# A scan's two terms: summed by GpSimd and turned once, with two operations moved by a step

## The chip, the cores and the metric

One core of a Trainium2 chip runs the kernel. The metric is device time in microseconds (us) of one execution. The engines are TensorE (PE; its weight loads are listed apart as PEld), VectorE (DVE), ScalarE (ACT), GpSimd (POOL) and SyncE (SP, which issues the DMAs).

## The reference

Four images of 128 channels and 64 x 64 pixels pass two layers. Only what matters here is kept:

```
# layer 0: state-space scan, per channel d (two chunks of 64 in one tile of 128 rows), 16 states n, 4096 pixels t
h[d, n] = exp(delta[d, t] * A[d, n]) * h[d, n] + delta[d, t] * B[n, t] * xin[d, t]
y[d, t] = sum over n of h[d, n] * C[n, t]
out     = (y + D * xin) * silu(z) @ out_proj        # then a norm, a projection, a residual
...
# layer 1: attention (4 heads of 32) over 4096 tokens, then a top-2 mixture of 8 experts
att = softmax(q @ k.T / sqrt(128)) @ v
```

The sum over the 16 states is where the change lies.

## The kernel before

**Tiles.** An image is 8 blocks of 512 pixels. A block has two halves p (two chunks each, 128 rows), and a half has 16 states, taken two at a time. A pair of states of one half is a unit; there are 4 x 8 x 2 x 8 = 512 units. VectorE runs both states of a unit in one scan over 1025 columns (`scan`), with the start of the second state put between them.

**The loop.** The main loop (from line 1291) goes in steps, which the code calls slots: two for each unit, so 1,024, and then more until the attention and the closing rows are through. The order of every engine's instructions is the order in which the loop issues them: line 445 is the helper that records each operation and ties it to the one before it on its engine, which is why nearly all rows of the profile have that line. A step issues:

- in an even step VectorE's product of rows and du into h (`driven`) and the scan of the unit; in an odd step `read`, which multiplies h by the rows of C into hc (128 x 2 x 512, two buffers);
- on ScalarE one half of the next unit's decays da (`decayed`, an exponential of 128 x 512), in odd steps the copy of one state into the next unit's h (`carried`), and two exponentials pT of 128 x 1024 for the attention (`exponentials`);
- on TensorE four score matmuls sc and, for the group of the step before, the weighted sums av (`weighted`);
- half steps of two lanes, X and Y, which hold all the rest as generators: each `yield` ends a half step. Y holds the norms, the convolution and the inputs of a block (`inputs`); X holds `closed` (what follows the scans of a block: projection, norm, keys, queries and values) and `finished` (task "out": attention's closing and the experts). Both keep their own order. A task "out" may start only in steps 2 to 17 of each 32; `closed` is put at the head of X's list by `summed_up` when the second half of its block is summed.

**The sum over states.** hc holds the terms of two states. Each term is turned by TensorE (`turned_on`, four transposes of 128 x 128 that accumulate in one PSUM tile y), so that TensorE adds up 16 terms. The first term of a unit is due one step after `read`, the second two steps after (line 1313 and 1314). After the last, ScalarE copies y to yT, a step later `turned_back` turns it back into the same PSUM buffer, and at once `summed_up` lets VectorE combine it with the input (xin <- xin, dsk, y) and GpSimd multiply it by the gate (zs).

**The state copy.** `kept` (ScalarE, 128 x 2) stores both last states of a unit's scan for the next block, 16 units later. It is issued at the end of the even step, the one that issues the scan.

**The start.** Attention needs finished blocks; its first group comes in step 80. ALONE is step 64 (two blocks).

Of the kernel before, what the change touches and what calls it, by code (L numbers as in the profile page):

```python
# [36 lines left out]
def conv_mamba_attn_moe_kernel(ctx: ExitStack, tc: tile.TileContext, t: dict):  # L37
# [401 lines left out]
    class Queue:  # L439
# [7 lines left out]
    tensor, vector, scalar, gpsimd, sync = (  # L447
        Queue(e) for e in (nc.tensor, nc.vector, nc.scalar, nc.gpsimd, nc.sync)
    )
# [14 lines left out]
    def flush():  # L464
        for entry in outgoing:
            entry[0] -= 1
            if entry[0] == 0:
                sync.dma_start(out=entry[1], in_=entry[2])
        outgoing[:] = [entry for entry in outgoing if entry[0]]
# [292 lines left out]
    def kept(unit, h):  # L762
        b, i, p, n = unit
        if i < NB - 1:
            scalar.copy(states[b % 2][:, p, n : n + 2], h[:, :, BLK - 1])

    def driven(unit, h, w):
        b, i, p, n = unit
        du = in_of[b, i, p][3]
        vector.tensor_mul(h[:, :, 0:BLK], w, du[:, None, :].to_broadcast([P, 2, BLK]))  # L770

    def scan(unit, h, da):

        b, i, p, n = unit
        h, da = (a.rearrange("p k q -> p (k q)")[:, 0 : 2 * BLK + 1] for a in (h, da))
        vector.tensor_tensor_scan(
            out=h, data0=da, data1=h, initial=states[b % 2][:, p, n : n + 1],
            op0=ALU.mult, op1=ALU.add,
        )

    def read(h, w):
        hc = mix.tile([P, 2, BLK], F32, name="hc", bufs=2)
        vector.tensor_mul(hc, w, h[:, :, 0:BLK])
        return hc

    def scanned(b, i, p, y):
        xin, zs, delta, du, bcd = in_of.pop((b, i, p))
        vector.scalar_tensor_tensor(xin, xin, dsk, y, ALU.mult, ALU.add)
        gpsimd.tensor_mul(zs, xin, zs)
        gated[b, i, p] = zs  # L790

    def turned_on(y, term, first, last):

        for j in range(NT):
            s = slice(j * P, (j + 1) * P)
            tensor.matmul(
                y[:, s], lhsT=term[:, s], rhs=ident, start=first and j == 0,
                stop=last and j == NT - 1, is_transpose=True,
            )

    def summed_up(b, i, p, y):
        scanned(b, i, p, y)
        done.add(("scan", b, i, p))
        if p == 1:
            lanes["X"].appendleft((("closed", b, i), closed(b, i), []))

    def turned_back(b, i, p, yT):
        y = ps_y.tile([P, BLK], F32, name="y")
        for j in range(NT):
            tensor.transpose(y[:, j * P : (j + 1) * P], yT[:, j * P : (j + 1) * P], ident)  # L810
        summed_up(b, i, p, y)

    vst = side.tile([P, NH, NT, 2 * DH], F32, name="vst")
    gpsimd.memset(vst[:, :, :, DH:], 1.0)
# [184 lines left out]
    sums, partial, total, inverse, later = [None], {}, {}, {}, deque()  # L999

    def exponentials(group):
        pTs = []
        for v, sc in group[3]:
            pT = att.tile([P, 2, BLK], F32, name="pT", bufs=4)
            scalar.activation(pT, sc, AF.Exp, scale=ATT_SCALE)
            pTs.append((v, pT))
        return *group[:3], pTs, *group[4:]
# [174 lines left out]
    lanes, done, running = {"X": deque(), "Y": deque()}, set(), {}  # L1182
# [3 lines left out]
    def advance(lane, second):  # L1186

        if inside[lane] != second:
            return False
        while True:  # L1190
            if lane not in running:

                tasks = lanes[lane] if lanes[lane] or slot < END else lanes["X"]
                if not tasks or not all(k in done for k in tasks[0][2]):
                    return False

                if (
                    tasks[0][0][0] == "out" and slot < END + 4
                    and not 2 <= slot % (2 * NST) < NST + 2
                ):  # L1200
                    return False
                key, stages, _ = tasks.popleft()
                running[lane] = key, stages(lane) if callable(stages) else stages
            key, stages = running[lane]
            try:
                next(stages)
                inside[lane] = not second
                return True
            except StopIteration:
                assert not second  # L1210
                done.add(key)
                del running[lane]

    def until(key):
        while key not in done:
            flush()
            count = len(done)
            moved = [
                advance(*half) for half in (("X", True), ("Y", False), ("Y", True), ("X", False))
            ]  # L1220
            assert any(moved) or len(done) > count, key
# [7 lines left out]
    X, Y = lanes["X"], lanes["Y"]  # L1229
# [9 lines left out]
    for k in range(-2, len(blocks)):  # L1239
        if 0 <= k:  # L1240
            b, i = blocks[k]
            Y.append((("in", b, i, 1), inputs(b, i, 1), [("scan", *blocks[k - 1], 1)] if k else []))
        if k + 2 < len(blocks):
            b, i = blocks[k + 2]
            if k + 2 == 0 or i > 0:
                upper(k + 2)
        if 0 <= k + 1 < len(blocks):
            b, i = blocks[k + 1]
# [10 lines left out]
    left = [None]  # L1259
# [8 lines left out]
    END = 2 * len(units)  # L1268

    ALONE = NB // 2 * NST  # L1270
    rows, due, closing, y_of = {}, deque(), deque(), {}
    h_of, slot = {}, 0

    def fetch(*wanted):
        for ahead, k in wanted:
            if ahead < len(units):
                until(("in", *units[ahead][:3]))
                rows[ahead, k] = fetched(units[ahead], k)

    def prepared(ahead, k):  # L1280
        if ahead < len(units):
            decayed(units[ahead], decays[ahead % 2], k)
            if k:
                h_of[ahead] = carried(units[ahead])

    def ends(unit):
        return unit[3] == NST - 2

    waiting = None

    while slot < END or due or closing or waiting or left or later or lanes["X"] or running:
        at, odd = divmod(slot, 2)
        flush()
        if slot == 0:
            fetch((0, 0), (0, 1), (1, 0))
            prepared(0, 0)
            prepared(0, 1)
        fetch((at + 2, 0) if odd else (at + 1, 1))
        unit = units[at] if at < len(units) else None
        prepared(at + 1, odd)  # L1300
        if unit and not odd:
            h = h_of.pop(at)
            driven(unit, h, rows.pop((at, 0)))
        advance("X", True)
        group = next(groups, None)
        if group:
            group = exponentials(group)
        if unit and not odd:
            scan(unit, h, decays[at % 2])
        if unit and odd:  # L1310
            hc = read(h, rows.pop((at, 1)))
            late = slot >= ALONE and unit[3] == 0
            due.append((slot + 1 + late, unit, 0, hc[:, 0, :], False))
            due.append((slot + 2, unit, 1, hc[:, 1, :], ends(unit)))
        advance("Y", False)
        while closing and closing[0][0] <= slot:
            turned_back(*closing.popleft()[1:])
        while due and due[0][0] <= slot:
            _, (b, i, p, n), k, term, done_with = due.popleft()
            first = n == 0 and k == 0  # L1320
            if first:
                y_of[b, i, p] = ps_y.tile([P, BLK], F32, name="y")
            turned_on(y_of[b, i, p], term, first, done_with)
            if done_with:
                yT = mix.tile([P, BLK], F32, name="yT")
                scalar.copy(yT, y_of.pop((b, i, p)))
                closing.append((slot + 1, b, i, p, yT))
        advance("Y", True)
        if unit and not odd:
            kept(unit, h)  # L1330
        if waiting:
            weighted(waiting)
        waiting = group
        advance("X", False)
        while later and later[0][0] <= slot:
            next(later.popleft()[1])
        slot += 1
# [113 lines left out]
```

## Time and profile before

| | us |
|---|---|
| three runs | 5374.57, 5390.83, 5391.15; median 5390.83 |
| profiled execution, its own time | 5380.67 |
| its span, first to last instruction | 5378.9 |
| first scan, last scan (start, from the span's start) | 101.1, 4787.7 |
| ScalarE idle before the state copies, all 448 | 416.3 |
| scan, mean of 512 | 2.491 |
| products h and hc, mean of 512 each | 1.382, 1.369 |
| GpSimd's adds avs <- avs, prev, mean of 96 | 1.594 |

How to read the profile: rows of groups give line, engine, operation, out<-in by tile names, count, busy time, mean of one, and the idle time of that engine just before them with what ended it. The view of waits sums those idle times by pairs (who waited for whom: total us, times, longest us). The view by windows gives busy us of each engine in stretches of the span, then the granted TensorE clock (1.00 is full), the DMA engines' share and GB/s. The timeline lists instructions in order of time: start, us, engine, line, operation, tiles, count. Matmuls are pipelined and their ends are modelled, so intervals between starts say more than their busy time. POOL's spans are rough.

### The profile page before, as it was taken

How to read it: one execution, taken by the hardware profiler on the slowest of the kernel's cores; microseconds unless marked ns; L12 is line 12 of the kernel's file. 1: busy time of each engine (PE TensorE's matmuls, PEld its weight loads, DVE VectorE, ACT ScalarE, POOL GpSimd, SP SyncE). 2: the span in 40 equal slices, each digit the busy share in tenths (PEclk: the TensorE clock that was granted, in tenths of full speed). 3: DMA queues.
4: the chain of work that ended last, by engine and by line, in shares of the span. 5: the costliest groups of instructions: out<-in, count | busy, mean ns of one | idle time of the engine just before them, and what ended most of it. 6: DMA issues, size and time to landing. Idle time of an engine off the chain costs nothing. (4 is left out here: it accounts for less than half of the span.)

```text
span 5378.9 us, 64061 instructions
## 1 busy us (share of the span) xinstructions
PE 4850.0 (90%) x21066; PEld 2366.3 (44%) x21066; DVE 3757.2 (70%) x5123; ACT 3926.8 (73%) x6117; POOL 1525.0 (28%) x1091
## 2 busy tenths in 40 slices
PE   4556898999999999999999999999999999999997
PEld 2333444444444444444444444444444444444443
DVE  4888767777777778877778778777777877751332
ACT  3456777888777788788877788787777787766553
POOL 2333233333322224223322324333322232310100
PEclk7677899999999999999999999999999999999998
DMA  3556567667666667666766667666766676655532
GB/s 95 176 186 208 197 205 242 231 228 240 232 209 215 218 218 258 225 223 233 257 216 213 217 221 251 233 207 240 270 205 202 207 237 218 239 191 174 174 138 70
DMA packets 451702, 1131.71 MB, mean 210 GB/s; under 512 B 51985, under 2 KB 135330, under 8 KB 451362
## 3 DMA queue, kind: packets, MB, share of 16 engines
q1 hardware_dynamic: 450194, 1126.74, 62.4%
q8 instruction: 169, 2.77, 0.2%
q14 instruction: 171, 1.40, 0.1%
q10 hardware_dynamic: 1168, 0.80, 0.0%
HBM read 967.12 MB, written 143.39 MB: 206 GB/s over the span
## 5 line engine op out<-in xcount | busy, mean ns | idle before, releaser
L445 ACT ACTIVATE pT<-sc 128x1024 f32<-128x1024 f32 x2048 | 1985.7, 1024 | 637.2 <-PE sc L445 635.5
L445 PE MATMUL av<-pT,v 128*64 128x512 f32 x8192 | 2011.1, 612 | 16.7 <-ACT avs L445 16.4
L445 PE MATMUL sc<-qs,ks 128*128 128x512 f32 x4096 | 1316.7, 440 | 134.4 <-ACT pT L445 82.1
L445 DVE TENSOR_TENSOR_SCAN h<-da,state,h 128x1025 f32<-128x1025 f32 x512 | 1275.5, 2491 | 198.2 <-ACT h L445 168.9
L445 PEld LDWEIGHTS sc<-qs,ks 128*128 128x128 f32 x4096 | 705.6, 192 | 835.6 <-ACT pT L445 376.0
L445 PEld LDWEIGHTS av<-pT,v 128*64 128x64 f32 x8192 | 503.4, 138 | 824.7 <-issue 780.0
L445 ACT ACTIVATE da<-delta,amat 128x512 f32<-128x512 f32 x1024 | 747.9, 731 | 4.5 <-POOL delta L445 2.6
L445 DVE TENSOR_TENSOR h<-rows,du 128x1024 f32<-128x1024 f32 x512 | 707.8, 1382 | 53.0 <-POOL du L445 28.5
L445 DVE TENSOR_TENSOR hc<-rows,h 128x1024 f32<-128x1024 f32 x512 | 700.9, 1369 | 18.2 <-PE y L445 4.4
L445 PE MATMUL y<-ident,hc 128*128 128x128 f32 x4096 | 639.5, 285 | 64.3 <-DVE hc L445 56.9
L445 PEld LDWEIGHTS y<-ident,hc 128*128 128x128 f32 x4096 | 523.5, 147 | 269.2 <-issue 116.7
L445 POOL TENSOR_TENSOR rsX<-rsX,mhalf 128x4 f32<-128x4 f32 x92 | 232.7, 2530 | 843.1 <-DVE shiftX L445 843.1
L445 ACT ACT_TABLE_LOAD x319 | 409.3, 1283 | 18.1 <-PE ps_Y L445 13.5
L445 POOL TENSOR_TENSOR rsY<-rsY,mhalf 128x4 f32<-128x4 f32 x100 | 171.5, 1715 | 795.7 <-DVE shiftY L445 795.7
L445 ACT COPY state<-h 128x2 f32<-128x2 f32 x448 | 87.8, 196 | 416.3 <-DVE h L445 412.4
L445 POOL TENSOR_TENSOR avs<-avs,prev 128x512 f32<-128x512 f32 x96 | 153.0, 1594 | 660.2 <-ACT avs L445 612.6
L445 POOL TENSOR_TENSOR zs<-xin,zs 128x512 f32<-128x512 f32 x64 | 105.0, 1640 | 806.5 <-DVE xin L445 797.2
L445 POOL TENSOR_SCALAR du<-e 128x512 f32<-128x512 f32 x64 | 130.3, 2035 | 554.6 <-ACT e L445 554.6
L445 DVE TENSOR_TENSOR share<-share,xf 128x1024 f32<-128x1024 f32 x128 | 177.9, 1390 | 150.9 <-DMA share<-sharesX 124.9
L445 PE MATMUL ps_X<-share,w_ew 128*128 128x512 f32 x432 | 214.5, 619 | 1.7
L445 DVE TENSOR_TENSOR res<-res,ps_X 128x512 f32<-128x512 f32 x108 | 73.4, 679 | 178.9 <-PE ps_X L445 126.9
L445 ACT ACTIVATE xt<-ps_Y,shiftY,rsY 128x128 f32<-128x128 f32 x380 | 143.0, 466 | 67.9 <-POOL shiftY L445 60.7
(238 smaller groups left out, 4415.9 us busy)
## 6 DMA issues: line engine op xcount, KB each, us to landing
rows<-bcd SPq DMA_DIRECT2D x1024, 512.0 KB
ks<-kd SPq DMA_DIRECT2D x192, 512.0 KB
qs<-qd SPq DMA_DIRECT2D x161, 512.0 KB
share<-sharesX SPq DMA_DIRECT2D x108, 512.0 KB
v<-vd SPq DMA_DIRECT2D x192, 256.0 KB
ks<-kd SPq DMA_DIRECT2D x128, 256.0 KB
avd<-avs SPq DMA_DIRECT2D x96, 256.0 KB
prev<-avd SPq DMA_DIRECT2D x96, 256.0 KB
```

The costliest lines, as they stand in the source:

```text
L445: return lambda *args, **kw: queued(op(*args, **kw))
```

## The change

From step 64 on, GpSimd adds the second term of hc to the first, in place, right after `read`, and only the sum is turned, two steps after `read` (three for the first unit of a half). Before step 64 both terms are turned as they were, with the first unit's two steps later. `kept` moves from the end of even steps to the end of odd ones. `turned_back` no longer calls `summed_up`; the loop calls it in the following step, after `driven` and ahead of lane X. Lane Y, which takes from X's list once the units are through, leaves a `closed` to X.

```diff
@@ turned_back
             tensor.transpose(y[:, j * P : (j + 1) * P], yT[:, j * P : (j + 1) * P], ident)
-        summed_up(b, i, p, y)
+        return b, i, p, y
@@ advance
                 tasks = lanes[lane] if lanes[lane] or slot < END else lanes["X"]
+                if tasks and lane == "Y" and tasks[0][0][0] == "closed":
+                    return False
@@ the main loop
-    waiting = None
+    waiting, summing = None, None
...
             driven(unit, h, rows.pop((at, 0)))
+        if summing:
+            summed_up(*summing)
+            summing = None
         advance("X", True)
...
             hc = read(h, rows.pop((at, 1)))
-            late = slot >= ALONE and unit[3] == 0
-            due.append((slot + 1 + late, unit, 0, hc[:, 0, :], False))
-            due.append((slot + 2, unit, 1, hc[:, 1, :], ends(unit)))
+            late = 2 * (unit[3] == 0)
+            if slot < ALONE:
+                due.append((slot + 1 + late, unit, 0, hc[:, 0, :], False))
+                due.append((slot + 2, unit, 1, hc[:, 1, :], ends(unit)))
+            else:
+                gpsimd.tensor_add(hc[:, 0, :], hc[:, 0, :], hc[:, 1, :])
+                due.append((slot + 2 + late // 2, unit, 0, hc[:, 0, :], ends(unit)))
         advance("Y", False)
         while closing and closing[0][0] <= slot:
-            turned_back(*closing.popleft()[1:])
+            summing = turned_back(*closing.popleft()[1:])
...
-        if unit and not odd:
+        if unit and odd:
             kept(unit, h)
```

More of the change, by code (lines that the diff above doesn't have):

```diff
@@ L1287, in ends @@
         return unit[3] == NST - 2
-    waiting = None
-    while slot < END or due or closing or waiting or left or later or lanes["X"] or running:
+    waiting, summing = None, None
+    while (
+        slot < END or due or closing or summing or waiting or left or later or lanes["X"] or running
+    ):
         at, odd = divmod(slot, 2)
```

## The prediction

> **What bounds the kernel now.** First the busy time by engine for the whole span, then the same busy times by stretch, because a mean hides stages with different limits.
>
> ```profile
> PE 4850.0 (90%) x21066; PEld 2366.3 (44%) x21066; DVE 3757.2 (70%) x5123; ACT 3926.8 (73%) x6117; POOL 1525.0 (28%) x1091
> ```
>
> ```profile
> core 0: us, PE busy (x) PEld busy (x) DVE busy (x) ACT busy (x) POOL busy (x), PEclk, DMA share, GB/s
> 100.00:323.00 223.00, 118.68 (x426) 72.45 (x426) 185.44 (x193) 112.83 (x225) 75.63 (x49) 0.67 0.51 171
> 323.00:700.00 377.00, 282.02 (x1156) 152.83 (x1156) 290.45 (x330) 247.57 (x432) 122.52 (x84) 0.84 0.62 204
> 700.00:1266.00 566.00, 530.31 (x2358) 255.87 (x2355) 407.28 (x472) 462.25 (x714) 186.80 (x129) 0.98 0.68 227
> 1266.00:4788.00 3522.00, 3329.12 (x14823) 1627.05 (x14822) 2698.26 (x3579) 2768.70 (x4327) 1081.15 (x741) 0.98 0.67 227
> ```
>
> Columns after the stretch: its length, busy us of PE, PEld, DVE, ACT, POOL. The reader is to see three stages. Until 323 us VectorE leads (185 of 223) and TensorE is half idle. To 700 us they cross. From there TensorE is busy 94%: it is the bound of 4,100 us. In the stretch 1266 to 4788, 370 pairs of scan states take 9.52 us each: 9.00 of TensorE, 7.29 of VectorE, 7.48 of ScalarE. After 4788 us (the last scan) only attention and the closing rows remain.
>
> **What a turn is worth on TensorE.** A turn of one term is four transposes. The group table puts 640 us on 4,096 of them, 0.62 us for four, but matmuls overlap. The tail's timeline, TensorE alone, has steps with a turn and one without:
>
> ```profile
> 4801.48 1.21 PE L445 MATMUL sc<-qs,ks 128*128 128x512 f32 x4
> 4802.52 0.60 PE L445 MATMUL y<-ident,yT 128*128 128x128 f32 x4
> 4803.05 1.94 PE L445 MATMUL av<-pT,v 128*64 128x512 f32 x8
> 4804.92 1.21 PE L445 MATMUL sc<-qs,ks 128*128 128x512 f32 x4
> 4806.06 1.94 PE L445 MATMUL av<-pT,v 128*64 128x512 f32 x8
> ```
>
> Scores to weighted sum: 1.57 us with a turn, 1.14 without. Over the whole trace the medians of that interval are 1.57 (547 steps with a turn alone) and 1.13 (95 with nothing between). A turn therefore costs **0.44 us**, not 0.62. The order in which the new program's instructions stand has 2,176 transposes of scan terms in place of 4,096, so 480 turns go. 48 of them lie in the pairs before about 700 us, where TensorE has gaps; 432 lie where it is the bound: 432 x 0.44 = **190 us** is the most that this can give.
>
> **What the add costs.** GpSimd has 480 new adds of 128x512. Its own time is cheap: the nearest rows (the adds of avs) have 1.26 us at least, and POOL is 31% busy. The price is paid by VectorE:
>
> ```profile
> 2047.93 1.72 POOL L445 TENSOR_TENSOR zs<-xin,zs 128x512 f32<-128x512 f32 x1 [10.34 <-DVE xin L445]
> 2048.43 2.30 DVE L445 TENSOR_TENSOR hc<-rows,h 128x1024 f32<-128x1024 f32 x1
> 2049.64 2.23 POOL L445 TENSOR_TENSOR avs<-avs,prev 128x512 f32<-128x512 f32 x1
> 2050.65 2.29 DVE L445 TENSOR_TENSOR h<-rows,du 128x1024 f32<-128x1024 f32 x1
> ```
>
> Alone, these two VectorE multiplies take 1.22 us (median of those with no POOL operation beside them); here 2.30 and 2.29, and the POOL add goes from 1.26 to 2.23. Sorted by what runs beside them, multiplies and scans lose about 1.0 us to a whole two-input 128x512 operation of GpSimd, and nothing to its small power operations. An add starts when the product hc ends; in the 1.3 us after that VectorE is busy 86% of the time in pairs 80 to 511 and 78% in pairs 32 to 79, with operands in SBUF. So an add takes about **0.88 us** of VectorE (bounds: 0 if it falls into idle time, 1.08 from the rows above).
>
> The add also brings a wait into GpSimd's queue: it stands there until hc is done, and behind it the lanes' power and shift operations (1.7 to 2.5 us and 0.3), for which ScalarE's xt waits. ScalarE waits 27.5 us for shiftX in the long stretch now; an add of 1.3 to 2.2 us ahead of them is inside the half to whole step that the lanes leave. In the other direction TensorE waits for the add, but takes its sum two steps (some 9 us) after hc. Only the five operations that end in du (9.5 us by their means in the group table, 64 times) can eat that; at worst 2 us each, +128, at best 0. I take 0: they are issued in an even step and leave the next add about 5 us.
>
> How much of the 0.88 shows? Eight equal stretches of block 18 (16 pairs, 2646 to 2798 us) have TensorE, VectorE, ScalarE at 19.0/13.5/16.7, 17.9/14.7/18.2, 17.6/14.9/15.6, 18.5/18.7/12.1, 16.8/12.7/15.0, 19.0/17.4/15.4, 19.0/8.5/16.5, 18.9/17.8/12.4 of 19.0. Take 0.88 from TensorE in each (two turns) and add 1.76 to VectorE. Averaged over the block VectorE has 132 against TensorE's 140, so everything is hidden: 27 blocks x 7.04 = -190. If instead each stretch goes by its own busiest engine, four gain 0.88, one (ScalarE's) nothing, and three turn to VectorE and lose 1.76, 0.11, 0.63: -1.0 a block, **-28**. The lanes hand tiles from TensorE to VectorE and back within half steps, so I stay nearer to the second end: **-80**.
>
> Pairs 32 to 79 run where VectorE leads: 48 x 0.78 = **+37** with almost nothing gained on TensorE.
>
> **The moved state copies.** The waits, for 1266 to 4788 us, ScalarE, VectorE and TensorE:
>
> ```profile
> ACT state L445 <- DVE h L445: 250.7, 110, 5.1
> ```
>
> ```profile
> DVE xin L445 <- PE y L445: 95.8, 44, 4.0
> ```
>
> ```profile
> PE sc L445 <- ACT pT L445: 61.2, 138, 3.0
> ```
>
> ScalarE waits for the scan with a 0.2 us copy (columns: total, times, longest), and the next decays, the copy into h and the exponentials stand behind it. One step later the scan is long done and the wait goes. What is late next is mostly TensorE's scores, for which ScalarE already waits 376 us in this stretch, so the 251 us are not the gain. TensorE's share is bounded by 0 and the 61 us that it waits for pT; I take half, **-30**. In the VectorE stage (100 to 700 us) ScalarE waits 142 us so and VectorE 53.9 us for the copy into h that is queued behind it: between 0 and -54, I take **-35**. The new copies sit ahead of the second half of lane X on ScalarE, as the old did; they read states first used 16 pairs later, so nothing waits for them.
>
> **The closing operation a step later.** xin has waited 96 us for the turned-back sum; a step later it does not wait. That gives VectorE cover (in the -80 already) and no time of its own. But it moves the lanes. A block's rows (task "out") may start at steps 2 to 17 of each 32. Before, the second sum closed in step 2 and put "closed" at the head of lane X, ahead of a waiting "out"; now it does so in step 3, when "out" has begun, and "closed" stands 16 steps behind it. Written out step by step from the two programs, batch 1's attention then finds its keys late at steps 411 to 415, 472 to 477 and 479 to 480, everything starts a step later, and the loop has 1,199 steps where it had 1,184. The 15 steps come back in the tail as attention alone, 1.14 + 1.87 = 3.01 us by the lines above: +45, less about 6 for the main steps that went without attention: **+39**. No DMA is added; those of "closed" move the 16 steps past the row loads on SP.
>
> Of the Trainium skill, "GPSIMD Engine Reference", section 4.1 Engine selection, speaks against the edit: it gives an elementwise add to VectorE and calls GpSimd about twice as slow for two inputs. The trace agrees on the ratio (1.26 us against 0.69 for aT, median, on VectorE). By that rule the add would cost VectorE 480 x 0.69 = 331 us directly, where the rows above make GpSimd's add cost it 480 x 0.88 = 422; the sum with the rule's choice would be between 0 and 91 us lower.
>
> **Sum.** 5380.7 (the profiled execution; span 5378.9) - 80 + 37 - 30 - 35 + 39 = **5312 us**, 1.3% lower; the median shown is 5390.8, 10 above that execution, inside the 16.6 us spread of the three.
>
> **Rivals.**
> (a) TensorE's relief comes through nearly whole: VectorE idles 824 us in the long stretch and the adds cost it 380 there. -190 - 61 - 54 + 37 + 39 gives 5152. Against it: VectorE's idle time is mostly waits for lane products, not free time. Chance 0.15.
> (b) VectorE becomes the bound, and the kernel is **slower**. Place: the stretches with the convolution's or "closed"'s VectorE work, three of the eight above. Price: their +2.5 a block, 27 blocks, +68, with the others' relief lost to TensorE waiting for lane products. 5380.7 + 68 + 37 + 39 - 65 = 5460. It decides once VectorE's 7.29 + 0.88 = 8.17 us of a pair pass some 95% of TensorE's 8.56 (9.00 less a turn); the quotient is 95%, so it stands at that point. Chance 0.31.
> (c) The parts cancel: uncovered contention, the 15 steps and the relief within 0.3% (16 us, about what a measurement of this kernel can tell from no change). 5381. Chance 0.12. That the turns stay is excluded by the order of the instructions.
> My forecast has 0.42. Faster: 0.42 + 0.15 = 0.57; same 0.12; slower 0.31. The range goes from 5230 (half of what lies between the forecast and (a)) to 5460 (b), leaving about 0.1 on each side.
>
> **What would show it.** Turns: 2,176 transposes of hc, TensorE's busy time down by about 300 us by the group table (0.62 a turn) though its interval shrinks by 0.44. Adds: 480 on POOL at 1.3 to 2.3 us; the mean of the multiplies up from 1.37 us, of the scan from 2.49, VectorE's busy time up by about 420 us. Copies: ACT's wait of state for h near nothing, xin's for y too. Steps: about 45 us more between the last scan and the end. I am wrong if VectorE passes 92% of the long stretch, if TensorE waits for hc (the add behind the five-operation du chain of 9.5 us on POOL), or if VectorE's busy time hardly grows.

## The result, and the profile after

The changed kernel takes **5406.95 us** (median of 7 runs, 5400.34 to 5430.06) against 5383.35 us (median of 7, 5374.57 to 5391.15): the ratio is **1.0054**, 95% interval 1.0042 to 1.0067. It is slower by about 0.5%, where 1.3% less was forecast. Its profiled execution took 5400.34 us, with a span of 5398.6.

The busy times by engine, then the same stretches by windows as before:

```profile
PE 4667.4 (86%) x19146; PEld 2141.1 (40%) x19146; DVE 3947.7 (73%) x5123; ACT 3919.5 (73%) x6117; POOL 2456.6 (46%) x1571
```

```profile
core 0: us, PE busy (x) PEld busy (x) DVE busy (x) ACT busy (x) POOL busy (x), PEclk, DMA share, GB/s
100.00:323.00 223.00, 118.95 (x436) 72.53 (x436) 193.02 (x195) 114.71 (x231) 76.98 (x50) 0.69 0.52 179
323.00:700.00 377.00, 248.26 (x906) 119.47 (x906) 303.05 (x322) 234.04 (x410) 206.38 (x129) 0.79 0.57 192
700.00:1266.00 566.00, 491.19 (x1973) 221.62 (x1972) 416.94 (x450) 427.14 (x662) 284.51 (x180) 0.92 0.64 214
1266.00:4788.00 3522.00, 3200.34 (x13467) 1464.34 (x13466) 2867.33 (x3623) 2790.86 (x4376) 1833.26 (x1127) 0.97 0.68 230
```

The turns are gone (19,146 matmuls where there were 21,066) and TensorE is busy 183 us less. But the span did not follow: TensorE is idle 5398.6 - 4667.4 = 731 us where it was idle 529. In the long stretch it is busy 91%, not 94.5%. VectorE has 169 us more work in that stretch, GpSimd 752.

Where in the run the time went is read from the starts of three scans:

| from, to | before | after | difference |
|---|---|---|---|
| start to pair 32 | 322.6 | 315.0 | -7.5 |
| pairs 32 to 160 | 1106.6 | 1152.4 | +45.8 |
| pair 160 to the last scan | 3358.5 | 3295.9 | -62.6 |
| last scan to the end | 591.2 | 635.2 | +44.0 |

So the late pairs gain, and two other stretches give back more. The last two rows belong together: attention's 1,024 groups (four score matmuls and eight weighted sums each) are all there in both, but 137 of them begin after the last scan before, and 152 in the changed kernel. Part of the 62.6 us is work that has moved to the tail. On TensorE, the timeline of the changed kernel has a step with a turn and one without:

```profile
3001.12 1.17 PE L445 MATMUL sc<-qs,ks 128*128 128x512 f32 x4
3002.13 0.60 PE L445 MATMUL y<-ident,hc 128*128 128x128 f32 x4
3002.66 1.94 PE L445 MATMUL av<-pT,v 128*64 128x512 f32 x8
3005.67 0.73 PE L445 MATMUL sc<-qs,ks 128*128 128x512 f32 x2 [1.07 <-ACT pT L445]
3006.58 0.73 PE L445 MATMUL sc<-qs,ks 128*128 128x512 f32 x2 [0.18 <-ACT pT L445]
3007.24 1.94 PE L445 MATMUL av<-pT,v 128*64 128x512 f32 x8
```

The step with a turn has its 1.54 us from scores to weighted sum. The one behind it has no turn, and yet takes 1.57: TensorE waits for pT, 1.07 us ahead of the first scores and 0.18 between them. The median of the interval is 1.13 without a turn and 1.56 with one, nearly as it was (1.13 and 1.57); the mean without one rose from 1.16 to 1.25.

The costliest groups that the change touches, and the waits of the whole execution (total us, times, longest):

```profile
L445 DVE TENSOR_TENSOR_SCAN h<-da,state,h 128x1025 f32<-128x1025 f32 x512 | 1399.5, 2733 | 103.1 <-ACT h L445 79.2
L445 POOL TENSOR_TENSOR hc<-hc 128x512 f32<-128x512 f32 x480 | 890.2, 1855 | 1165.0 <-DVE hc L445 1056.4
```

```profile
ACT pT L445 <- PE sc L445: 726.2, 538, 10.0
...
ACT xt L445 <- POOL shiftX L445: 123.5, 24, 12.4
PE ps_X L445 <- ACT xt L445: 109.8, 19, 13.9
ACT state L445 <- DVE h L445: 87.4, 32, 7.5
PE sc L445 <- ACT pT L445: 71.9, 138, 3.0
PE y L445 <- POOL hc L445: 67.2, 29, 14.4
```

The add takes 1.86 us on GpSimd and the scan went from 2.49 to 2.73 us. Over the whole span VectorE is busy 190 us longer (3947.7 against 3757.2), which is 0.40 us an add. ScalarE waits for the scan 87 us where it was 412, and for the scores 726 where it was 636: part of that time only moved over to the next waits. Two of TensorE's waits are new or larger: it waits for xt 110 us (57 before), up to 14 us at once, and for the add's sum 67 us, where it waited 57 us for hc itself before (and still 37). ScalarE's xt waits for GpSimd's shift 124 us (38 before); but that wait is 152 us in e6 below too, which moves only the state copies, so it says nothing of the add or the closing.

### The profile page after: what moved, and what is told of

It reads as the page before. It is cut to its first block, busy times and chain, and to the rows that moved or that the text cites. A ratio compares the mean times of both kernels' runs of the same rounds, so it can differ in the third digit from the quotient of the medians.

```text
span 5398.6 us, 61313 instructions
## 1 busy us (share of the span) xinstructions
PE 4667.4 (86%) x19146; PEld 2141.1 (40%) x19146; DVE 3947.7 (73%) x5123; ACT 3919.5 (73%) x6117; POOL 2456.6 (46%) x1571
## 5 line engine op out<-in xcount | busy, mean ns | idle before, releaser
L445 DVE TENSOR_TENSOR_SCAN h<-da,state,h 128x1025 f32<-128x1025 f32 x512 | 1399.5, 2733 | 103.1 <-ACT h L445 79.2
L445 POOL TENSOR_TENSOR hc<-hc 128x512 f32<-128x512 f32 x480 | 890.2, 1855 | 1165.0 <-DVE hc L445 1056.4
L445 DVE TENSOR_TENSOR h<-rows,du 128x1024 f32<-128x1024 f32 x512 | 743.5, 1452 | 50.8 <-POOL du L445 25.8
L445 DVE TENSOR_TENSOR hc<-rows,h 128x1024 f32<-128x1024 f32 x512 | 671.2, 1311 | 57.0 <-DVE h L445 20.3
L445 PE MATMUL y<-ident,hc 128*128 128x128 f32 x2176 | 357.7, 293 | 104.4 <-POOL hc L445 67.2
L445 PEld LDWEIGHTS y<-ident,hc 128*128 128x128 f32 x2176 | 290.6, 152 | 228.2 <-POOL hc L445 83.6
L445 POOL TENSOR_TENSOR rsX<-rsX,mhalf 128x4 f32<-128x4 f32 x92 | 201.2, 2187 | 348.7 <-DVE shiftX L445 348.5
L445 POOL TENSOR_TENSOR zs<-xin,zs 128x512 f32<-128x512 f32 x64 | 140.2, 2190 | 211.0 <-DVE xin L445 211.0
L445 POOL TENSOR_SCALAR du<-e 128x512 f32<-128x512 f32 x64 | 168.5, 2633 | 115.8 <-ACT e L445 115.8
L445 DVE SCALAR_TENSOR_TENSOR cm<-y,w_fc1w,cm 128x512 f32<-128x512 f32 x192 | 189.7, 988 | 3.4
```

Source lines behind the costliest of these rows:

```text
L445: return lambda *args, **kw: queued(op(*args, **kw))
```

## The experiments

All medians below stand beside 5381 us for the kernel before in the same runs (5380.9 to 5381.4), and ratios have their 95% intervals. "At once" and "later" say in which step the closing operation stands. Unless it says otherwise a kernel is the changed one with the edit shown.

### First four: the lane's order, the moves alone, and the add's engine and length

**e1**: `closed` keeps its place ahead of "out", so that the loop has 1,185 steps instead of 1,199.

```diff
-                    and not 2 <= slot % (2 * NST) < NST + 2
+                    and not 4 <= slot % (2 * NST) < NST + 2
```

> The changed kernel, except that a task 'out' may start at steps 4 to 17 of each 32 instead of 2 to 17, so that 'closed' is in lane X before it; the loop has 1,185 steps instead of 1,199. Theory A (most of the loss is the 15 steps that the later closing operation pushed into the tail, 44 us more there between last scan and end in the two traces): 5407 - 45 = about 5362, 0.4% below the kernel before. Rival B (the steps are neutral, because attention that is missing in the main stage makes it shorter there; the loss is GpSimd's adds): about 5400, slower than before as the change is.

Measured: **5528.39**, ratio 1.0274 (1.0260 to 1.0289). Both theories fell: without the 15 steps the kernel is 121 us slower than the change. The reason shows in every block of e1 but the last; in the changed kernel it shows only in the first nine, up to 1,355 us, and in one later block:

```profile
1658.79 2.12 POOL L445 TENSOR_TENSOR hc<-hc 128x512 f32<-128x512 f32 x1 [6.46 <-DVE hc L445]
1660.88 1.93 POOL L445 TENSOR_SCALAR du<-e 128x512 f32<-128x512 f32 x1
...
1669.28 2.12 POOL L445 TENSOR_TENSOR du<-delta,xin 128x512 f32<-128x512 f32 x1
1671.37 3.02 POOL L445 TENSOR_TENSOR rsX<-rsX,mhalf 128x4 f32<-128x4 f32 x1
...
1674.70 1.50 ACT L445 ACTIVATE xt<-ps_X,shiftX,rsX 128x128 f32<-128x128 f32 x4 [9.35 <-POOL shiftX L445]
...
1676.26 1.12 PE L445 MATMUL ps_X<-ident,xt 128*128 128x128 f32 x4 [8.04 <-ACT xt L445]
```

This is e1's timeline, GpSimd's rows first. The add waits 6.46 us for hc at the head of GpSimd's queue; the five-operation du chain, whose input e ScalarE had finished at 1655.7, starts only at 1660.9; rsX, whose input VectorE had ready at 1662.2, starts at 1671.4. ScalarE then stands 9.35 us ahead of xt, with the exponentials behind it, and TensorE stands still for 8.04. (Three of the chain's five operations are left out above.) In the traces, the first rsX of `closed` stands right ahead of the du chain on GpSimd in 31 blocks of the kernel before, and right behind it in 31 of e1: the later closing moved the norm of `closed` by one step, behind the chain. In the changed kernel it stands right behind the chain in ten blocks; in nearly all others `closed` runs half a block later, and its rsX comes some 57 to 79 us behind that chain.

**e2**: e1 with both terms turned everywhere (no sum).

```diff
-            if slot < ALONE:
+            if True:
```

> As e1, but the pair sum is left out everywhere: both terms are turned, as before, with the state copies and the closing operation moved as in the change. Theory A, by the prediction's terms (-30 and -35 for the copies): about 5318, and faster than e1 if the adds cost more than the turns that they save. Rival B (the moved copies free no engine that is late, ScalarE's wait goes over to the scores): within 0.3% of the kernel before, 5370 to 5400.

Measured: **5360.10**, 0.9965 (0.9951 to 0.9978): a gain, but a third of theory A's.

**e3**: e1 with the adds on VectorE.

```diff
-                gpsimd.tensor_add(hc[:, 0, :], hc[:, 0, :], hc[:, 1, :])
+                vector.tensor_add(hc[:, 0, :], hc[:, 0, :], hc[:, 1, :])
```

> As e1, with the 480 adds on VectorE instead of GpSimd. By the traces GpSimd's add takes 0.77 us from VectorE (its excess beside the 474 adds that stand alone in the changed kernel's trace), 368 us in all; an own add of 128x512 takes 0.69 us, 331 us. Theory A (the price of an add is VectorE time): 5 to 40 us below e1. Rival B (VectorE in its own order is the bound, an add there delays everything behind it, one on GpSimd only half): above e1 by 20 to 100 us. Theory C (the price is GpSimd's queue, where lane operations stand behind an add that waits for hc): below e1 by 50 us or more, because that queue is then as short as before.

Measured: **5373.74**, 0.9987 (0.9978 to 0.9996), 155 us below e1: theory C. The du chain has the same place in front of rsX, but nothing holds it up.

**e4**: e1 with the add on 4 of 512 columns (`hc[:, 0, 0:4]` and so on); the other 508 columns of the second terms are left out.

> As e1, with GpSimd's add on 4 of 512 columns; the sum of the terms is left out for the other 508, so the second terms are missing. The wait for hc in GpSimd's queue stays, its length and what it takes from VectorE go. Theory A (contention is the price): 368 us of VectorE return and TensorE's relief comes through, 5150 to 5230. Theory C (the wait in the queue is the price, not the length): within 30 us of e1.

Measured: **5441.01**, 1.0114 (1.0098 to 1.0129). Neither number: 87 us below e1, so the add's length counts (its time on GpSimd, what it takes from VectorE, or both), and 81 above e2 though 480 turns are gone, so the bare wait in the queue counts as well. At this point I held that GpSimd's queue was the whole loss (theory Q), and the next four were to show it.

### Second four: the closing at once

**e5**: the closing operation back in the step of the turned-back sum; 1,184 steps, rsX ahead of the chain in 31 blocks.

```diff
-            summing = turned_back(*closing.popleft()[1:])
+            summed_up(*turned_back(*closing.popleft()[1:]))
```

> The changed kernel with the closing operation back in the step of the turned-back sum; sum on GpSimd and moved copies stay. Theory Q (the later closing puts lane X's first power operation rsX of 'closed' behind the five-operation du chain in GpSimd's queue; the adds, which wait for hc, hold that chain up and lengthen it, ScalarE's xt waits and TensorE with it): rsX stands ahead of the chain again, as in the kernel before, TensorE's wait of ps_X for xt falls from 110 us (264 in e1) to about 57, the 15 steps go too: 5300 to 5345. Rival V (VectorE's lost time by the adds is the price, wherever the closing lies): 5385 to 5420, and VectorE's wait of xin for y, 125 us before, comes back on top.

Measured: **5419.58**, 1.0070 (1.0054 to 1.0085). Theory Q falls as the whole cause: with the queue in order and no steps lost the sum is still slow, as rival V had it.

**e6**: the kernel before with the state copies alone moved.

```diff
-        if unit and not odd:
+        if unit and odd:
             kept(unit, h)
```

> The kernel before with the state copies alone moved to the end of odd steps. Theory Q: e2 (copies and closing moved, no sum, 5360) less what the closing's place cost there (TensorE's wait of ps_X for xt 99 us against 57 before): 5318 to 5345. Rival V (the copies give nothing, e2's gain was the closing's, VectorE no longer waiting for the turned sum): 5370 to 5395.

Measured: **5388.95**, 1.0012 (1.0003 to 1.0022). ScalarE's two waits, first before and then in e6:

```profile
ACT state L445 <- DVE h L445: 412.4, 157, 7.9
ACT pT L445 <- PE sc L445: 635.5, 499, 9.3
```

```profile
ACT state L445 <- DVE h L445: 53.4, 22, 4.6
ACT pT L445 <- PE sc L445: 791.2, 556, 9.3
```

The wait for the scan falls by 359 us; the wait for the scores grows by 156, and that of xt for GpSimd's shift from 38 to 152. The copies give nothing.

**e7**: e5 with the adds on VectorE, as e3.

> As e5 with the adds on VectorE. Theory Q: GpSimd's queue no longer matters once rsX is ahead of the chain, so it is within 30 us of e5, by VectorE's 331 us against the 368 that GpSimd's adds take a little below it: 5290 to 5340. Rival V (VectorE is the bound): as e3, 5360 to 5390.

Measured: **5428.85**, 1.0093 (1.0075 to 1.0112). It is within 30 us of e5 as theory Q said, but both numbers are on rival V's side or beyond it. For the kernel it hardly counts whether VectorE adds itself or GpSimd does, although VectorE's busy time differs: 4155.0 us here, 3995.8 in e5.

**e8**: e5 with the copies in even steps, so the sum alone.

> The sum on GpSimd alone: copies at the end of even steps and closing at once, as before. Theory Q: e5 plus what the copies give (some 40 us by e2): 5340 to 5385. Rival V: the sum alone costs more than its turns save, 5400 to 5440.

Measured: **5410.68**, 1.0045 (1.0030 to 1.0061): the sum costs 30 us. (e5 against e6 says 31.) Both kernels with the sum also turn a half's first unit a step later than the kernels without it; no run has that alone.

### Third four: what the turns are worth and what the adds cost

**e9**: e5 with e4's 4 columns (the same part of the sum left out).

> e5 (sum on GpSimd, copies moved, closing at once) with the add on 4 of 512 columns; the sum is left out for the other 508, so most of the second terms are missing. Theory S (VectorE is full in stretches of 5 us and more, 1,320 us of them in e5 against 1,010 in e6, and what the adds take from it there stops TensorE): VectorE gets 368 us back, 5270 to 5330. Theory W (the wait in GpSimd's queue is the price): 5395 to 5420, as e5. Theory K (TensorE's removed work was only cover for the lanes' chain of TensorE, VectorE, GpSimd and ScalarE, which paces the steps): 5370 to 5400, as e6.

Measured: **5286.40**, 0.9818 (0.9802 to 0.9834), as theory S had it. VectorE's busy time falls from 3995.8 us in e5 to 3690.4.

**e10**: e5 without the add; every second term is left out.

```diff
-                gpsimd.tensor_add(hc[:, 0, :], hc[:, 0, :], hc[:, 1, :])
```

> e5 without any add: only the first term of each pair is turned, the second is left out, so this prices the 480 missing turns alone. Theory S and theory W: the relief of up to 190 us comes through but for what the lanes keep, 5220 to 5310. Theory K: within 30 us of e6, 5360 to 5400.

Measured: **5290.40**, 0.9833 (0.9815 to 0.9851), the same as e9 within 4 us: with the closing at once the wait in GpSimd's queue costs nothing. Against e6 this prices 480 missing turns at 5388.95 - 5290.40 = **99 us**, and e5 against e9 prices the length of the adds at 5419.58 - 5286.40 = **133 us**.

How the 133 us come about is seen in the long stretch of e5 and then of e9, and in the scan's row of each:

```profile
1266.00:4788.00 3522.00, 3227.25 (x13253) 1466.30 (x13253) 2865.56 (x3563) 2749.39 (x4312) 1783.17 (x1107) 0.96 0.66 225
```

```profile
1266.00:4788.00 3522.00, 3284.73 (x13667) 1497.51 (x13667) 2663.91 (x3656) 2804.74 (x4385) 1363.64 (x1121) 0.97 0.69 231
```

```profile
L445 DVE TENSOR_TENSOR_SCAN h<-da,state,h 128x1025 f32<-128x1025 f32 x512 | 1443.5, 2819 | 121.8 <-ACT h L445 88.4
```

```profile
L445 DVE TENSOR_TENSOR_SCAN h<-da,state,h 128x1025 f32<-128x1025 f32 x512 | 1255.4, 2452 | 143.6 <-ACT h L445 111.7
```

VectorE's share of 3522 us is 81% in e5 and 76% in e9, which looks harmless. It is not spread evenly. Ten-microsecond windows of e5 around 2,450 us:

```profile
2430.00:2440.00 10.00, 9.24 (x46) 5.07 (x48) 9.82 (x10) 6.55 (x12) 2.80 (x2) 1.00 1.03 353
2440.00:2450.00 10.00, 6.59 (x28) 4.12 (x26) 9.93 (x11) 3.97 (x7) 2.46 (x2) 0.83 0.79 273
2450.00:2460.00 10.00, 7.49 (x31) 3.18 (x28) 9.83 (x23) 6.41 (x16) 6.72 (x5) 0.93 0.78 264
2460.00:2470.00 10.00, 10.00 (x38) 4.61 (x37) 4.52 (x8) 9.37 (x14) 3.83 (x3) 0.73 0.30 110
```

VectorE (third number) is full for 30 us on end, TensorE (first) falls to 6.6 and 7.5 of 10, and the granted clock to 0.73 in the window after. Counting windows of 5 us from 1266 to 4640 us in which VectorE is busy at least 97%: 1,090 us of them in e6, 1,435 in e5, 1,070 in e9 (e9's expectation had 1,010 and 1,320 for the first two); TensorE's idle time inside them is 75, 163 and 90 us. On top of that TensorE's own work gets slower: the same 8,192 weighted sums are busy 2,014 us in e6, 2,054 in e5 and 2,038 in e9. The profiled executions of e5 and e9 are 117 us apart; 63 of these are idle time of TensorE and 53 are longer busy time.

The price of the adds' length is shown; the way it is paid is shown only in part. e9 shortens what the adds take from VectorE and what they take up in GpSimd's queue together. TensorE waits 46 us for the add in e5 and 25 in e9, so the queue can hold a share; e7, which has no adds there, is as slow as e5. No run separates the two.

**e11**: the sum's turn a step later, in even steps.

```diff
-                due.append((slot + 2 + late // 2, unit, 0, hc[:, 0, :], ends(unit)))
+                due.append((slot + 3 - ends(unit), unit, 0, hc[:, 0, :], ends(unit)))
```

> e5 with the sum's turn in the even step after (three steps after hc instead of two, except for the last pair of a half). In e5 the steps with a turn, the odd ones, take 5.06 us with 0.66 of TensorE idle, those without 4.76 with 0.35. Theory P (the turn sits in the steps that VectorE's hc and the add hold up; in the others TensorE's room is free): 20 to 60 us below e5. Theories S, W and K: within 15 us of e5.

Measured: **5431.49**, 1.0084 (1.0067 to 1.0102). Theory P falls: the parity of the turn is not it (12 us above e5).

**e12**: e2 with the copies in even steps, so the later closing alone.

> The kernel before with the closing operation a step later (and 'out' from step 4 on, both terms turned), copies at the end of even steps. e2 had the copies moved as well and took 5360; e6 had the copies alone and took 5389. If the parts add up: e2 less what the copies cost alone (8 us): 5345 to 5360. If the later closing only pays together with the moved copies: 5375 to 5395.

Measured: **5348.22**, 0.9929 (0.9912 to 0.9947): the parts add up, and the later closing, with "out" held back to step 4, is worth 33 us. This kernel also turns the first term of a half a step later than the kernel before; no run separates that.

### Last three: is it the order in GpSimd's queue?

The later closing gains 33 us without the sum and loses 109 with it (e1 against e5). The edit, in `inputs`, ahead of the du chain:

```diff
         yield
         yield
+        yield
+        yield
 
         du = mix.tile([P, BLK], F32, name="du", bufs=2)
```

**e13**: e1 with it; rsX stands ahead of the chain again in 31 blocks.

> e1 (5528) with the five-operation du chain issued one step later (two more yields of lane Y ahead of it), so that rsX of 'closed' stands ahead of it in GpSimd's queue in 31 blocks, where e1 has none. Theory Q (the order of these two in GpSimd's queue, with the adds ahead, is what the later closing costs: e1's TensorE waits 264 us for xt): 5360 to 5430, and that wait under 120 us. Rival (the later closing costs by anything else, VectorE's share or the lanes' half steps): 5490 to 5540.

Measured: **5367.20**, 0.9970 (0.9958 to 0.9982), 161 us below e1. TensorE's wait for xt, first e1, then e13:

```profile
PE ps_X L445 <- ACT xt L445: 263.7, 38, 14.0
```

```profile
PE ps_X L445 <- ACT xt L445: 35.5, 15, 6.5
```

That is theory Q, within its limits: issuing the chain a step later, which puts rsX ahead of it again, is worth 161 us there.

**e14**: the changed kernel with it.

> The changed kernel (5407, 1,199 steps) with the chain one step later; rsX ahead of it in 34 blocks instead of 24. Theory Q: the stalls of 7 to 14 us in the blocks without a task 'out' go (TensorE waits 110 us for xt, 57 before): 5330 to 5380. Rival: 5395 to 5420.

Measured: **5449.50**, 1.0133 (1.0116 to 1.0149). A miss: 43 us slower than the changed kernel. Half of the expectation holds: from pair 32 to pair 160, where no "out" stands ahead of `closed`, the time falls from 1152 to 1100 us. From pair 160 to the last scan it grows from 3296 to 3396 us. There `closed` runs 16 steps later and rsX did not stand right behind the chain (the expectation counts 24 and 34 blocks with rsX ahead; the traces have it right behind the chain in ten blocks of the changed kernel and in none of e14). So there was almost nothing to mend there, and the chain's later step costs 100 us instead. TensorE's waits for xt in lane Y (130 us, 80 in the changed kernel), for ScalarE's zs (62 against 22), for pT (97 against 72) and for the add (88 against 67) all grow. Which of them comes first is not settled.

**e15**: e12 with it.

> e12 (closing later, no sum, copies as before, 5348) with the chain one step later. Theory Q: without adds the chain starts early and costs little, so 10 to 30 us less, 5318 to 5340 (TensorE waits 97 us for xt in e12, 57 before). Rival: within 8 us of e12.

Measured: **5310.52**, 0.9873 (0.9857 to 0.9889), 38 us below e12, more than theory Q's 10 to 30; TensorE's wait for xt falls from 102 to 38 us. This kernel leaves nothing out, has no sum, and is faster than both kernels: 1.3% below the kernel before. With the sum and the moved copies the same kernel is e13, 57 us slower.

## Why the prediction was wrong, point by point

**The turn.** Right in size: 0.43 us of interval, 480 gone. TensorE's busy time fell by 183 us, not by the 300 that the prediction gave as a sign. Too high in effect: the term allowed up to 190, and e10 against e6 shows 99 with no add in the way. The rest went into TensorE's idle time (520 us in e6, 595 in e10).

**The add.** The direction was right, the size per add too high. VectorE's busy time grows by 190 us in the changed kernel, 0.40 an add, where 0.88 and about 420 us were forecast. e5 against e10, which has no adds, gives 228 us (3995.8 - 3767.5), 0.48 each; against e9 it is 305 us, 0.64 each. VectorE's share of the long stretch is 81%, under the 92% that the prediction set as a sign of being wrong, and yet it holds TensorE up. Two shares that went into the 0.88 were also read a little low: after hc VectorE is busy 89% and 81% of the 1.3 us in the trace before, not 86% and 78%.

**The step that failed** is the one that set relief and loss against each other, "I stay nearer to the second end: **-80**", with +37 for the early pairs: -43 together. The runs show **+30** (e8), from -99 for the turns and +133 for the adds (at e5's place). The +37 was too much: pairs 32 to 79 take 3 us longer in e5 than in e6, and 7 longer in e8 than before. The -80 had the wrong sign: from pair 80 to the last scan, where TensorE was said to be the bound, e5 takes 23 us longer than e6 and e8 28 longer than before. The working had the sign at hand, because three of its eight stretches turned to VectorE, and e5's full windows show the loss in such stretches. It took the relief elsewhere as whole, where e10 gives half of it, and it left out that the same TensorE work takes longer in the kernels with the sum (the weighted sums: 2,014 us in e6, 2,032 in e10, 2,054 in e5). This was rival (b), with its price too high: it had +68 and +37 for the sum, which costs 30 us.

**The copies** failed by as much: -30 and -35 were forecast, and +8 (e6) and +12 (e2 against e12) measured. ScalarE's wait for the scan did go, as said, and later waits, the scores' first, took over a large part of it. Counting half of TensorE's wait for pT as gain was the wrong step, since that wait stayed (82 us before, 81 in e6). So did most of VectorE's wait for the copy into h, which the -35 rested on: 53.9 us from 100 to 700 us before, 43.3 in e6.

**The closing**, +39 for the 15 steps: the tail grew by 44 us, as worked out. But the term stopped at the steps. It missed that the later closing is worth 33 us without the sum (e12), and that it puts rsX behind the du chain. The prediction looked at that chain only for TensorE's wait for the add and set it to nothing. That wait came, 67 us in the changed kernel, which is one of the prediction's own signs of being wrong; a second one came by ScalarE's xt. In the changed kernel the second falls on the early pairs: pairs 32 to 160 take 46 us longer than before, and 53 us less in e14, where the order in the queue is put right.

**The sum.** With the measured parts: sum +31 and copies +8 give e5's 5420; the later closing, with its 15 steps, its stalls in the early blocks and its gain in the late ones (-63 us against before, from pair 160 on), takes 13 off: 5407. The gain in the late pairs is in part attention that moved out of them: 15 groups at 3.01 us are 45, by an estimate from the prediction's tail lines, and the tail grew by 44. What the late blocks gain beyond that when "out" runs ahead of `closed` is not separated by any run; e14 shows that it hangs on the same lane timing.

## What to carry to other kernels

Work that is moved off the bounding engine is worth only what the next engine leaves, so add the moved work to that engine stretch by stretch, and believe the stretches rather than their mean. An engine with a share of 46% of the span can still hold the kernel up by the order of its queue: for each instruction that is added or moved, list what stands behind it and when that was ready. And where a change bundles several edits, price them apart: here one of three, the later closing, was a gain that the other two hid.

## What the runs showed of the hardware that was not expected

An add on GpSimd cost this kernel about as much as the same add done by VectorE itself: e5 and e7 differ by 9 us, although VectorE's busy time is 228 us above e10's in e5 and 388 in e7. The page "GPSIMD Engine Reference" of the Trainium skill, section 4.1, prefers VectorE; with the queue out of order that held by 155 us (e1 against e3), with the queue in order not at all.

Where TensorE stalls, its granted clock is lower in these traces. In the 10 us windows of e5 from 700 to 4780 us the clock is 0.98 on average where TensorE is idle less than 0.5 us (233 windows) and 0.83 where it is idle 3 us or more (23 windows); before it is 1.00 (268) and 0.84 (11). The mean granted clock was 0.951 before, 0.936 after and 0.923 in e1, and the same weighted sums were busy 2,011 us, 2,022 and 2,054. That the stall is the cause was not tried apart.
